# Two convolution blocks in one kernel: another order of work at the seams between its passes

## The chip, the cores and the metric

The kernel runs on one core of one Trainium2 chip. A core has a matrix engine (TensorE, PE in the profile, with weight loads listed apart as PEld), a vector engine (VectorE, DVE), an activation engine (ScalarE, ACT), a general engine (GpSimd, POOL) and a queue engine (SyncE, SP) that only issues transfers. Each engine works through its own instructions in order. Transfers are issued from SP, ACT or POOL and run on 16 DMA engines. The metric is the time of one execution on the device, in microseconds (us); lower is better.

## The reference, cut to what matters

The input x is an image batch of shape (8, 96, 96, 192) in f32. Two layers follow each other, both with a residual sum:

```python
x = x + L0(group_norm(x, 32 groups))      # layer 0
x = x + L1(group_norm(x, 32 groups))      # layer 1

def L0(x):                                # 192 -> 384 -> 192 channels
    proj  = x @ W_in + b_in
    local = depthwise_conv_3x3(proj)
    # s = 0.6 s + 0.4 v, along the width and the height, both ways
    mixed = 0.25 * (lr + rl + tb + bt) + local
    return (layer_norm(mixed) * ln_g + ln_b) @ W_out + b_out

def L1(x):                                # 192 -> 768 -> 192 channels
    y = depthwise_conv_7x7(x) + dw_bias
    y = layer_norm(y) * ln_gamma + ln_beta
    y = gelu(y @ w0 + b0)
    return (y @ w1 + b1) * gamma
```

Group norm needs the mean and the variance of a whole image over six channels before it can scale the first value, so layer 1 cannot begin with an image before layer 0 is done with it.

## The kernel before, in words

The work is cut into passes; what one pass leaves for the next goes through DRAM in another layout.

The **first pass** (0 to about 770 us) normalises x, multiplies by W_in and writes P_d.

The **second pass** (770 to 1,820 us) goes over the 384 channels in 96 steps of four (k), each in three parts (i). A part is loaded (`load_b`), convolved 3x3 on TensorE (`conv_b`), scanned down and up on VectorE (`scan_down`, `scan_up`), mixed on TensorE (`mix_b`), and the scans are added to the mix by GpSimd (`add`, L672). The mix of a step trails its convolution by one step. Every second step, a tile mo of 8 channels is full, and eight transfers (`store_steps`, L655) write it to M_d, two per part of the following step, all issued by GpSimd. After the last step the rest is issued at once.

The **third pass** (1,842 to 2,652 us) takes 192 units, one image column and one half of the batch each. `load_c` loads mt (the column of M_d, all 384 channels, 576 KB) and xr (the column of x, 288 KB), three units ahead, on SP. `block_c` transposes and multiplies by W_out on TensorE, `finish_c` scales and adds x. Sixteen units fill a tile x1c, which is stored to X1_d by twelve transfers (`store_c`, L1034) on SP, one per unit; after the last unit all twelve go out together. Statistics for layer 1's group norm are taken on the way. For the first half of the batch they are finished inside the pass; for the second half by the six steps of `norm_c(1)` later. Twenty units before the end, band 0 and raw 0, the first inputs of the 7x7 convolution, are loaded.

The **7x7 convolution** has 32 steps: two batch halves times 16 groups of 12 channels (`todo`). A step needs the following:
- `load_raw(n, t)`, t = 0 to 2: one tile of X1_d each, of which SP and GpSimd load 64 partitions each (384 KB a half).
- `load_band(n)`: the band matrices (624 KB) for 64 partitions, by SP for an even n and by GpSimd for an odd one; VectorE copies them to the other 64 (`spread`, L817).
- `scale_steps(n)`: 24 scale operations (L806) from raw into xin, the group norm, and `spread` behind them.
- `conv_d(n, c)`, c = 0 to 5: 24 matmul instructions (L1131) and two ScalarE evictions into yo.
- `store_d(n)`: six transfers into Y_d, half of them on SP and half on GpSimd.

Tiles alternate between two pools, `early` and `d_own`, so that a step's inputs load while the step before computes; d_own opens after the third pass, in memory that the third pass used, and raw 1 belongs to early. Steps 0 to N1 - 1 run in a loop of their own ahead of the last pass; the other steps are cut into nine slots each and run inside the last pass's first half.

The **last pass** (3,010 us to the end) has 72 units (u), two per tile y. `load_y` reads Y_d (four transfers on SP), `load_r` reads X1_d for the residual, and GpSimd adds the bias to it (`bias_r`, L1190). `prepare` and the pieces of it in the loop take the layer norm's statistics and write yn on VectorE, with a power on GpSimd (L29). `turn_in(u, k)` transposes yn on TensorE (L1226) into the only buffer of its PSUM pool, and VectorE copies that to yT (L1229). `first_layer` multiplies by w0 (L1244, L1254), with Gelu on ScalarE; `second_layer` multiplies by w1 (L1274), and VectorE adds the residual (L1285). Unit u's first layer stands beside unit u - 1's second layer. In the first half (`early_half`) a unit's first layer comes in three parts with five PSUM banks, in the second in two parts.

The order is written out by hand: inside a block opened by `tc.manual_schedule()` each engine gets its instructions in the order of the source. Between blocks, instructions of a later one can move up where an engine would be free: SP issues its halves of raw 1 at 2,616 and 2,635 us, inside the third pass. Waits are put in by the framework, by tile.

Of the kernel before, what the change touches and what calls it, by code (L numbers as in the profile page):

```python
# [101 lines left out]
def conv_blocks_kernel(  # L102
# [51 lines left out]
    M_d = dram.tile([S, C, B, S], F32, name="M_d")  # L154
# [406 lines left out]
    with ExitStack() as ph:  # L561
# [81 lines left out]
        def store_steps(mo, o):  # L643

            steps = []
            for i in range(NI):
                runs = []
                for at, (c, j) in enumerate(place[i]):
                    if runs and runs[-1][1] == c:
                        runs[-1][3] += 1  # L650
                    else:
                        runs.append([at, c, j, 1])
                for at, c, j, n in runs:
                    steps.append(
                        lambda i=i, at=at, c=c, j=j, n=n: nc.gpsimd.dma_start(  # L655
                            M_d[
                                j * RB : (j + n) * RB, o * 2 * CC + c : (o + 1) * 2 * CC : CC
                            ].rearrange("w c b h -> w c (b h)"),
                            mo[at * RB : (at + n) * RB, :, i].rearrange("p k q n -> p k (q n)"),
                        )  # L660
                    )
            return steps

        n_k = C // CC
        with tc.manual_schedule():
# [3 lines left out]
            def add(k, i):  # L669
                m = mos[k // 2][:, k % 2, i].rearrange("p q (j n) -> p q j n", j=3)  # L670
                z = zs.pop((k, i)).rearrange("p q (n j) -> p q j n", j=3)
                nc.gpsimd.tensor_tensor(m, m, z, ALU.add)  # L672

            up_next = None
            for n in range(NI * (n_k + 1)):
# [18 lines left out]
                if k:  # L694
# [7 lines left out]
                    if k % 2 and i == NI - 1:  # L702
                        todo += store_steps(mos.pop(k // 2), k // 2)
# [57 lines left out]
    N1 = NI + 2  # L761
# [33 lines left out]
    def scale_steps(n):  # L795
# [4 lines left out]
        def scale(t, k, b):  # L800
            if (t, k, b) == (0, 0, 0):
# [4 lines left out]
            nc.vector.tensor_scalar(  # L806
                xins[n][:, t, b, c].rearrange("q c (a v) -> q a c v", a=NV),
                raws[n, t][:, b, :, c],
                sc,
                sh,  # L810
                ALU.mult,
                ALU.add,
            )
# [86 lines left out]
    with ExitStack() as ph:  # L900
# [48 lines left out]
        M_f = M_d.rearrange("w c b h -> w c (b h)")  # L949
# [6 lines left out]
        def load_c(u):  # L956
# [4 lines left out]
            nc.sync.dma_start(  # L961
                mt,
                M_f[S - 1 - w, :, hf * NH * S : (hf + 1) * NH * S].rearrange(
                    "(m c) n -> c m n", c=128
                ),
            )
# [487 lines left out]
```

## Time and profile before

| what | us |
|---|---|
| median of three runs | 5,662.74 (5,660.78 to 5,672.44) |
| the profiled execution's own time | 5,654.68 |
| its span, first to last instruction | 5,652.9 |
| TensorE busy | 5,393.8 (95% of the span) |
| VectorE, ScalarE, GpSimd busy | 3,066.6, 2,233.1, 2,103.9 |
| first matmul of the third pass (L979) | at 1,841.5 |
| first matmul of convolution step 1 (L1131) | at 2,696.3 |
| first matmul of the last pass's first layer (L1244) | at 3,016.3 |

The mean granted TensorE clock is 0.979 of full speed. The profile's rows are read like this: a number of an L is a line of the kernel; `out<-in` names the tiles that an instruction writes and reads; an arrow with an engine and a line names what ended a wait. In the slices the span is cut into 40 equal parts of 141 us, and a digit is the busy share in tenths. In a timeline row the first number is the start and the second the length from the first to the last instruction of a merged group, and the brackets give the idle time of the engine before it. A releaser is inferred, and where a wait had several causes the last one is named.

### The profile page before, as it was taken

The page shows a single profiled execution, that of the slowest core. Times are in us where ns is not written, and L with a number is a line of the kernel's source. Part 1 is how long each engine was busy: PE and PEld are TensorE (multiplying, and loading weights), DVE is VectorE, ACT ScalarE, POOL GpSimd, SP SyncE. Part 2 cuts the span into 40 slices and gives each one's busy share as a digit, 9 for nine tenths or more (in the row PEclk, how much of TensorE's full clock was granted, in tenths as well). Part 3 has the DMA queues.
Part 4 walks back from the last instruction along what each step waited for, and adds up shares of the span by engine and source line. Part 5 has one row for each costly group of instructions (what it writes and reads, how often), then busy time and mean ns, then how long its engine had stood idle before and what let it go on. Part 6 is the DMA issues. An engine that isn't in the chain of part 4 may idle for free.

```text
span 5652.9 us, 106714 instructions
## 1 busy us (share of the span) xinstructions
PE 5393.8 (95%) x43070; PEld 3443.0 (61%) x43070; DVE 3066.6 (54%) x6353; ACT 2233.1 (40%) x5282; POOL 2103.9 (37%) x2093
## 2 busy tenths in 40 slices
PE   5999989999998999997688999999999999999999
PEld 3666643333332999997344666666666667676777
DVE  5556449999998455554545444444333334333332
ACT  2444447777775566564232222222222222222221
POOL 1111128888888555554222222222222222222221
PEclk9999989999999999999789999999999999999999
DMA  7999869999997899999898456555332222322321
GB/s 200 283 285 272 238 196 243 243 245 242 244 246 206 256 285 289 281 288 265 217 274 196 117 106 129 126 126 123 86 74 67 69 69 69 80 69 69 72 65 40
DMA packets 695589, 996.62 MB, mean 176 GB/s; under 512 B 234343, under 2 KB 576920, under 8 KB 693048
## 3 DMA queue, kind: packets, MB, share of 16 engines
q1 hardware_dynamic: 598600, 620.64, 44.8%
q0 software_dynamic: 90368, 366.55, 20.8%
q8 instruction: 340, 5.57, 0.4%
q10 hardware_dynamic: 6128, 2.61, 0.2%
q14 instruction: 153, 1.25, 0.1%
HBM read 585.22 MB, written 419.95 MB: 178 GB/s over the span
## 4 chain that ended last, share of the span: by engine, by line
PE 77%; DMA 4%; issue 2%; DVE 2%; POOL 1%; SPq 0%; ACT 0%; POOLq 0%; DVEq 0%; ACTq 0%
PE hp L1274 19%; PE hp L1244 13%; PE pl L599 11%; PE po L981 11%; PE hp L1254 7%; PE pa L620 5%; PE hp L1131 4%; PE pt L979 3%; PE pa L623 2%; PE pt L1226 2%; DMA raw<-X 1%; DMA band<-Z_d 1%; DVE xin L806 1%; DMA Y<-yo 1%; DMA mt<-M_d 0%
## 5 line engine op out<-in xcount | busy, mean ns | idle before, releaser
L1274 PE MATMUL hp<-w1g,g 128*128 128x192 f32 x6912 | 1170.8, 328 | 4.0 <-DVE xo L1285 4.0
L1263 ACT ACTIVATE g<-hp,b0g 128x512 f32<-128x512 f32 x864 | 519.8, 692 | 1641.9 <-PE hp L1254 1641.9
L1274 PEld LDWEIGHTS hp<-w1g,g 128*128 128x128 f32 x6912 | 1121.2, 190 | 68.6 <-issue 42.5
L1293 POOL DMA_DIRECT2D out_dram<-xo x288 | 211.3, 734 | 1613.9 <-DVE xo L1285 1579.6
L1244 PE MATMUL hp<-yT,w0w 128*128 128x512 f32 x1728 | 779.3, 597 | 0.0
L981 PE MATMUL po<-wc,mt 128*128 128x193 f32 x3456 | 685.0, 334 | 1.8 <-DVE x1c L998 1.8
L599 PE MATMUL pl<-pin,band 34*32 34x380 f32 (+1 forms) x13824 | 631.1, 490 | 18.8 <-DMA pin<-P_d 18.5
L1285 DVE TENSOR_TENSOR xo<-hp,r 128x384 f32<-128x384 f32 x288 | 230.6, 801 | 739.3 <-PE hp L1274 739.3
L672 POOL TENSOR_TENSOR mo<-mo,z 128x768 f32<-128x768 f32 x288 | 602.1, 2091 | 2.9 <-ACT mo L624 0.4
L981 PEld LDWEIGHTS po<-wc,mt 128*128 128x128 f32 x3456 | 554.8, 191 | 32.3 <-ACT mean L983 30.1
L1229 DVE COPY yT<-pt 128x512 f32<-128x512 f32 x216 | 148.8, 689 | 749.6 <-PE pt L1226 749.5
L1244 PEld LDWEIGHTS hp<-yT,w0w 128*128 128x128 f32 x1728 | 320.3, 191 | 358.4 <-issue 353.4
L632 DVE TENSOR_TENSOR_SCAN z<-decay,loc 128x768 f32<-128x768 f32 x288 | 505.9, 1756 | 45.4 <-ACT loc L608 16.7
L1131 PE MATMUL hp<-xin,band 63*64 63x372 f32 (+1 forms) x4608 | 430.0, 509 | 101.2 <-DVE band L817 51.8
L641 DVE TENSOR_TENSOR_SCAN z<-decay,z 128x768 f32<-128x768 f32 x288 | 498.4, 1731 | 0.1
L599 PEld LDWEIGHTS pl<-pin,band 34*32 34x32 f32 x13824 | 232.5, 107 | 399.1 <-issue 398.2
L1141 ACT ACTIVATE yo<-hp,dwb 128x384 f32<-128x384 f32 x384 | 202.2, 578 | 608.2 <-PE hp L1131 443.2
L620 PE MATMUL pa<-loc,mix 128*32 128x384 f32 x3456 | 432.8, 494 | 0.0
L623 PE MATMUL pa<-last,down 96*32 96x384 f32 x1152 | 427.7, 494 | 0.9 <-ACT mo L624 0.9
L1254 PE MATMUL hp<-yT,w0w 64*128 64x512 f32 x1728 | 419.5, 611 | 0.0
L381 PE MATMUL pm<-xT,win 128*128 128x384 f32 x1152 | 394.4, 493 | 8.0 <-DVE po L405 8.0
L1131 PEld LDWEIGHTS hp<-xin,band 63*64 63x64 f32 x4608 | 211.6, 141 | 278.7 <-issue 244.7
(141 smaller groups left out, 6674.4 us busy)
## 6 DMA issues: line engine op xcount, KB each, us to landing
P_d<-po POOLq DMA_DIRECT2D x96, 1152.0 KB, 9.8
pin<-P_d SPq DMA_DIRECT2D x192, 576.0 KB
mt<-M_d SPq DMA_DIRECT2D x192, 576.0 KB
xq<-in_x_dram SPq DMA_DIRECT2D x96, 576.0 KB
xr<-in_x_dram SPq DMA_DIRECT2D x192, 288.0 KB
X<-x1c SPq DMA_DIRECT2D x144, 384.0 KB
y<-Y SPq DMA_DIRECT2D x144, 384.0 KB
r<-X SPq DMA_DIRECT2D x36, 1536.0 KB
```

Of the source, the lines that this page charges most:

```text
L599: nc.tensor.matmul(pls[g][at * RB : (at + 1) * RB, :, lo:hi], band[rows, c, kh, :], pin[rows, c, :, NJ - 1 - j, lo + kh - 1 : hi + kh - 1] ...
L620: nc.tensor.matmul(pa[at], mix[:, i, at], loc[:, q], start=True, stop=True)
L623: nc.tensor.matmul(pa[at], down[:, to], last[:, q], start=True, stop=True)
L632: nc.vector.tensor_tensor_scan(zf, decay_f, loc.rearrange("p q n -> p (q n)"), 0.0, ALU.mult, ALU.add)
L641: nc.vector.tensor_tensor_scan(zr, decay_f, zr, 0.0, ALU.mult, ALU.add)
L672: nc.gpsimd.tensor_tensor(m, m, z, ALU.add)
L981: nc.tensor.matmul(po, lhs[m], wc[:, m], start=(m == 0), stop=(m == NC - 1))
L1131: nc.tensor.matmul(pys[g][k * 64 : (k + 1) * 64, :, lo:hi], band[rows, k * GS + c, d * ZS : d * ZS + 64], xin[rows, :, :, k * GS + c, lo + ...
L1244: nc.tensor.matmul(hps[m, q], w0w[:, 2 * q, m * 128 : (m + 1) * 128], yT[:, 2 * q], start=True, stop=False,)
L1254: nc.tensor.matmul(hps[m, q], w0w[p, 1, m * 128 : (m + 1) * 128], yT[p, 1], start=False, stop=True,)
L1263: nc.scalar.activation(g[:, m, q], hps[m, q], AF.Gelu, bias=b0g[:, m : m + 1], scale=1.0)
L1274: nc.tensor.matmul(po[:, q], g[:, m, q, k * 128 : (k + 1) * 128], w1g[:, m], start=(m == 0), stop=(m == NE - 1),)
```

## The change

It moves work over the seams between the passes, and changes two tensors and a count.

- M_d becomes two DRAM tensors, one for the first 256 channels and one for the last 128, and `load_c` loads mt with two transfers.
- In the second pass's last step, VectorE does the adds of parts 1 and 2 in place of GpSimd, and each part's stores are issued right behind its add, by SP and GpSimd in turn.
- `load_raw(1, t)` moves from the start of the convolution's loop to the end of the third pass, ahead of its last stores; step 1's scale operations move from VectorE to ScalarE.
- N1 is 19 instead of 18, so one step more runs ahead of the last pass. `load_y(1)`, the next step's band and its raw move behind the last convolution of that loop; `load_y(0)` stays at step 16, and `prepare(0)` at the last step.
- The six steps of `norm_c(1)` go one by one to steps 3 to 8 instead of three each to steps 1 and 2; `make_weights` goes from step 2 to step 10, ahead of the scale operations.
- In the last pass slots begin with unit 2 instead of unit 0, `load_y(2)` stands behind `prepare(1)`, and in the first half `turn_in(u + 1, 1)` stands ahead of `second_layer(u - 1, 1)` instead of behind it.

The core of the diff (the loop that builds the runs in `store_steps` is only un-nested):

```diff
-    M_d = dram.tile([S, C, B, S], F32, name="M_d")
+    CS = 2 * C // 3
+    M_d = [dram.tile([S, n, B, S], F32, name=f"M_{n}") for n in (CS, C - CS)]
...
-        def store_steps(mo, o):
+        def store_steps(mo, o, i, engs=(nc.gpsimd,)):
+
+            m, lo = divmod(o * 2 * CC, CS)
...
+            for at, c, j, n in runs:
+                eng = engs[len(steps) % len(engs)]
+                steps.append(
+                    lambda eng=eng, at=at, c=c, j=j, n=n: eng.dma_start(
+                        M_d[m][
+                            j * RB : (j + n) * RB, lo + c : lo + 2 * CC : CC
+                        ].rearrange("w c b h -> w c (b h)"),
+                        mo[at * RB : (at + n) * RB, :, i].rearrange("p k q n -> p k (q n)"),
                     )
+                )
...
-                nc.gpsimd.tensor_tensor(m, m, z, ALU.add)
+                eng = nc.vector if k == n_k - 1 and i else nc.gpsimd
+                eng.tensor_tensor(m, m, z, ALU.add)
...
-                    if k % 2 and i == NI - 1:
-                        todo += store_steps(mos.pop(k // 2), k // 2)
+                    if k == n_k - 1:
+                        for step in todo + store_steps(
+                            mos[k // 2], k // 2, i, (nc.sync, nc.gpsimd)
+                        ):
+                            step()
+                        todo = []
+                    elif k % 2 and i == NI - 1:
+                        for i in range(NI):
+                            todo += store_steps(mos[k // 2], k // 2, i)
...
-    N1 = NI + 2
+    N1 = NI + 3
...
-            nc.vector.tensor_scalar(
-                xins[n][:, t, b, c].rearrange("q c (a v) -> q a c v", a=NV),
-                raws[n, t][:, b, :, c],
-                sc,
-                sh,
-                ALU.mult,
-                ALU.add,
-            )
+            to = xins[n][:, t, b, c].rearrange("q c (a v) -> q a c v", a=NV)
+            of = raws[n, t][:, b, :, c]
+            if n == 1:
+                nc.scalar.activation(to, of, AF.Identity, bias=sh, scale=sc)
+            else:
+                nc.vector.tensor_scalar(to, of, sc, sh, ALU.mult, ALU.add)
...
-            nc.sync.dma_start(
-                mt,
-                M_f[S - 1 - w, :, hf * NH * S : (hf + 1) * NH * S].rearrange(
-                    "(m c) n -> c m n", c=128
-                ),
-            )
+            for f, m in zip(M_f, (slice(0, CS // 128), slice(CS // 128, NC))):
+                nc.sync.dma_start(
+                    mt[:, m],
+                    f[S - 1 - w, :, hf * NH * S : (hf + 1) * NH * S].rearrange(
+                        "(m c) n -> c m n", c=128
+                    ),
+                )
...
                 held = (pos, var, xr) if u < n_u else None
+            for t in range(NT):
+                load_raw(1, t)
             for store in stores:
                 store()
...
             load_band(1)
-            for t in range(NT):
-                load_raw(1, t)
             norms = norm_c(1, bank)
             for n in range(N1):
                 if n:
                     store_d(n - 1)
-                    load_band(n + 1)
+                    if n + 1 < N1:
+                        load_band(n + 1)
                 if n == NI:
                     load_y(0)
-                    load_y(1)
+                if n >= 3 and norms:
+                    norms.pop(0)()
+                if n == 10:
+                    make_weights(bank())
                 if n == N1 - 1:
-                    for t in range(NT):
-                        load_raw(N1, t)
                     prepare(0)
...
-                if n == 2:
-                    make_weights(bank())
                 for c in range(GS):
                     conv_d(n, c)
-                    if 0 < n < 3 and c % 2:
-                        norms.pop(0)()
+            load_y(1)
             store_d(N1 - 1)
+            load_band(N1)
+            for t in range(NT):
+                load_raw(N1, t)
...
-            if slots:
+            if slots and u >= 2:
                 for step in slots.pop(0):
                     step()

         load_r(0)
-        load_y(2)
         for k in range(3):
             turn_in(0, k)
         prepare(1)
+        load_y(2)
...
             if early_half:
                 first_layer(u, 1, parts, pool)
+                turn_in(u + 1, 1)
             second_layer(u - 1, 1, pool)
-            turn_in(u + 1, 1) if u < n_u else None
+            if not early_half and u < n_u:
+                turn_in(u + 1, 1)
             slot()
```

More of the change, by code (lines that the diff above doesn't have):

```diff
@@ L641, in scan_up @@
             nc.vector.tensor_tensor_scan(zr, decay_f, zr, 0.0, ALU.mult, ALU.add)
-        def store_steps(mo, o):
[L645 to L659, printed above, removed]
-                        )
+        def store_steps(mo, o, i, engs=(nc.gpsimd,)):
+            m, lo = divmod(o * 2 * CC, CS)
+            runs, steps = [], []
+            for at, (c, j) in enumerate(place[i]):
+                if runs and runs[-1][1] == c:
+                    runs[-1][3] += 1
+                else:
+                    runs.append([at, c, j, 1])
+            for at, c, j, n in runs:
[6 more added lines that the diff above has]
+                        mo[at * RB : (at + n) * RB, :, i].rearrange("p k q n -> p k (q n)"),
                     )
+                )
             return steps
@@ L805, in scale @@
             sc, sh = (s1[:, hf, b, e, 2 * i + k : 2 * i + k + 1] for e in range(2))
-            nc.vector.tensor_scalar(
-                xins[n][:, t, b, c].rearrange("q c (a v) -> q a c v", a=NV),
-                raws[n, t][:, b, :, c],
-                sc,
-                sh,
-                ALU.mult,
-                ALU.add,
-            )
+            to = xins[n][:, t, b, c].rearrange("q c (a v) -> q a c v", a=NV)
+            of = raws[n, t][:, b, :, c]
+            if n == 1:
+                nc.scalar.activation(to, of, AF.Identity, bias=sh, scale=sc)
+            else:
+                nc.vector.tensor_scalar(to, of, sc, sh, ALU.mult, ALU.add)
         def spread():
@@ L947, in conv_blocks_kernel @@
             nc.vector.tensor_tensor(cst, bo, ps[:, D : 2 * D], ALU.add)
-        M_f = M_d.rearrange("w c b h -> w c (b h)")
+        M_f = [m.rearrange("w c b h -> w c (b h)") for m in M_d]
         x_f = x.rearrange("b h w c -> (b h) w c")
@@ L960, in load_c @@
             mt = ip.tile([128, NC, NH * S], F32, tag="mt", name="mt")
-            nc.sync.dma_start(
-                mt,
-                M_f[S - 1 - w, :, hf * NH * S : (hf + 1) * NH * S].rearrange(
-                    "(m c) n -> c m n", c=128
-                ),
-            )
+            for f, m in zip(M_f, (slice(0, CS // 128), slice(CS // 128, NC))):
[5 more added lines that the diff above has]
+                )
             xr = ip.tile([128, NJ3, D], F32, tag="xr", name="xr", bufs=5)
```

## The prediction

> **What bounds the kernel now.** I read the page's slices first: which engine is full where.
>
> ```profile
> PE   5999989999998999997688999999999999999999
> PEclk9999989999999999999789999999999999999999
> DMA  7999869999997899999898456555332222322321
> ```
>
> TensorE is full nearly everywhere. The one hole wider than a slice lies in slices 18 to 21, 2,650 to 3,010 us, where the first 18 of the 32 steps of the 7x7 convolution run alone; there DMA is full instead. So an edit is worth what it takes out of a TensorE wait, and in that hole what it takes out of a DMA gap. The table of waits, TensorE only, says which waits exist (total, times, longest):
>
> ```profile
> PE hp L1131 <- DVE band L817: 51.8, 10, 30.1
> PE hp L1131 <- DMA band<-Z_d: 35.7, 6, 8.5
> PE pt L979 <- DMA mt<-M_d: 28.7, 2, 21.2
> PE pt L1226 <- DVE yT L1229: 21.7, 21, 1.2
> PE hp L1131 <- DVE b0g L748: 9.3, 1, 9.3
> ```
>
> The change touches every one of these five. The same hole cut by time (time; busy of TensorE, weight loads, VectorE, ScalarE, GpSimd; clock; DMA share; GB/s):
>
> ```profile
> 2651.00:2768.00 117.00, 64.70 (x611) 33.20 (x612) 54.05 (x155) 25.27 (x48) 26.17 (x34) 0.75 0.78 197
> 2768.00:2980.00 212.00, 165.01 (x1750) 98.46 (x1752) 104.62 (x303) 75.81 (x144) 50.88 (x76) 0.87 1.01 275
> ```
>
> From step 4 on DMA is saturated at 275 GB/s and a step takes 17.3 us (from L1131's starts at 2767.6 and 2975.5, twelve steps), against 11.7 us of matmuls in a row. In the first 117 us DMA moves only 197 GB/s: that stretch is slack, not throughput.
>
> **1. End of the second pass.** GpSimd's timeline, and from the chain that ended last the third pass's first matmuls:
>
> ```profile
> 1813.12 5.98 POOL L672 TENSOR_TENSOR mo<-mo,z 128x768 f32<-128x768 f32 x3
> 1819.05 4.51 POOL L655 DMA_DIRECT2D M_d<-mo  x8
> ...
> 1841.47 0.90 PE pt L979 x3
> ```
>
> Three adds, then eight store issues, all on GpSimd; the chain then shows 9.3 us for the stores to land and 8.8 us for the first load of mt. After the change GpSimd has one of these adds, ending at 1815.2; VectorE, free of scans at 1811.1, does the other two. A 128x384 add of theirs (L859) takes 0.56 us, so 768 elements about 1 us each: done at 1813.1. Eight issues over two queues, five on SP and three on GpSimd at 0.56 us, end about 1818 instead of 1823.6. SP is free for them, having issued nothing since 1772. But the stores' 2.36 MB and 2 MB of weight loads already fill DMA until 1831, so landing gains about 4 us, not 5.6. Then only the last third of mt (192 KB) waits for it; the first two thirds are older and load meanwhile: 2 to 3 us more. Sum by the rows: -7 us.
>
> Here a rule speaks against the edit. A row shows VectorE and GpSimd in each other's way: eight scale operations, first without and then under a GpSimd operation of 5.44 us (L1190, started at 3242.67):
>
> ```profile
> 2771.72 2.41 DVE L806 TENSOR_SCALAR xin<-raw,s 128x192 f32<-128x192 f32 x8 [2.79 <-DMA raw<-X]
> ...
> 3242.12 8.13 DVE L806 TENSOR_SCALAR xin<-raw,s 128x192 f32<-128x192 f32 x8
> ```
>
> The Trainium skill (GPSIMD Engine Reference, 1. Specifications) says that GpSimd shares its SBUF interfaces with VectorE and contends with instructions that have two SBUF inputs, which these adds are. By the rule the adds run one after the other, about 2 us later, and the sum is -5. I take -6; bounds 0 and -11.
>
> **2. mt by two loads.** 192 more DMAs in the third pass (1,842 to 2,649 us, 4.13 us a unit, TensorE full, DMA 0.93 at 283 GB/s). SP issues mt in 0.36, xr in 0.55, a store in 0.60 us: with 0.4 more that is 1.9 of 4.13. The cover is a prefetch of three units. The rule against it: the skill (DMA: Bandwidth & Descriptors, Anatomy of one DMA) gives a fixed 2.0 us a DMA; exposed, 192 of them would be +384 us. But mt's loads carry such latencies already, and TensorE waited for mt just twice in the pass, so it is hidden unless it occupies the DMA engines. Bound for that: a unit moves 1.18 MB, which at 283/0.93 = 304 GB/s needs 3.88 us, slack 0.25. The second pass with its many small transfers (237 GB/s at share 0.91) keeps the engines 1.4 us longer per channel step of 10.9 us than 304 GB/s would, over 12 DMAs: 0.12 us each. Below 0.25: cost 0.
>
> **3. Start of the convolution.** TensorE's and GpSimd's rows:
>
> ```profile
> 2652.95 13.29 PE L1131 MATMUL hp<-xin,band 63*64 63x384 f32 x142 [2.77 <-DVE x1c L998]
> 2696.33 6.80 PE L1131 MATMUL hp<-xin,band 63*64 63x384 f32 x48 [30.09 <-DVE band L817]
> ...
> 2672.90 0.57 POOL L790 DMA_DIRECT2D band<-Z_d  x1 [21.40 <-DMA Y<-yo]
> 2673.47 3.74 POOL L780 DMA_DIRECT2D raw<-X  x6
> ```
>
> GpSimd's halves of step 1's raw stand behind the band load, which waits for memory that the third pass's last stores (4.7 MB, landing about 2,670) still hold. So VectorE scales at 2,687, and only then copies the band. Moved ahead of those stores, GpSimd's three issues go out at 2,651; SP's three went at 2,616 and 2,635 and stay. ScalarE scales as they land: 24 operations of about 0.37 us (0.16 for one element, L983, and 0.58 for 384, L985, give the line), 8.9 us. What queues behind: step 0's evictions on ScalarE, so step 0 ends near 2,675 instead of 2,667; nothing waits for that, as DMA is busy with the stores. The stores land some 4 us later for sharing; the band issues about 2,677 and lands about 2,684, and step 1 begins about 2,686, 10 us earlier. Then group norm and weight scaling leave steps 1 and 2, where they cost twice: 2.5 and 9.3 us of TensorE waits, and late stores behind which SP held the next loads (DMA share 0.07 in 2,710 to 2,720, 0.13 in 2,740 to 2,750). Spread over steps 3 to 8 and 10 they meet 17.3 - 11.7 = 5.6 us of idle TensorE a step; weight scaling takes 3.8 us of matmuls there, and VectorE reaches it ahead of the next band. GpSimd's powers (5.62 us) delays half a prefetched raw. The bytes check it: 23.0 MB in 2,651 to 2,768 take 84 us at 275 GB/s, 33 less than 117. I take -30; bounds -10 (step 1 alone) and -36.
>
> **4. A 19th step ahead of the last pass.** It adds 4.77 MB (raw 2.36, band 0.64, stores 1.77), 17.3 us at the stage's pace; out of the stage go y 1, the next band and raw, 4.6 MB. The end is a chain, not throughput. Count from step 15's start (before: 2,958.6). Its store lands about +32 (before +30; half a raw more beside it). SP, which waits there, then issues y 0 (1.57 MB), its half of raw 18, its half of store 16 and band 18: 5.2 MB, landed at +52. Copy, step 18 from +53.5 to +65.5, then three transposes with copies: first MLP matmul at +69.5. Before it came at 3,016.3, +57.7. So +11.8. y 0's statistics fit under step 18. Bounds +5 and +25.
>
> **5. The last pass.** One convolution step less inside: six pieces of 2.06 us (between neighbouring starts at 3,229.0 and 3,231.1), -12.4. And the moved turn_in:
>
> ```profile
> 4111.71 0.60 PE L1226 MATMUL pt<-ident,yn 128*128 128x128 f32 x4
> 4113.36 0.66 PE L1226 MATMUL pt<-ident,yn 128*128 128x128 f32 x4 [1.06 <-DVE yT L1229]
> ```
>
> Turns 1 and 2 follow each other and share one PSUM buffer; after 3,062 us this wait occurs 18 times, 19.0 us. With 4.1 us of second layer between them the 0.69 us copy is done. I take -19; bounds -21 and -10 (were VectorE late there). Next in line is the bank wait on L1285, 4.0 us in all, unchanged. The entry: before it idles 5.8 us after the first matmul and loses 3 to a cold clock (0.53 in 3,010 to 3,020). After, units 0 and 1 have no convolution to fill: 3.7 us for unit 1's yn, 1.1 for a turn pair, and about 5 for unit 2's yn, since GpSimd waits for r 0 before bias_r (5.4 us) and its power stands behind: +1 net, bounds -4 and +10. Slots 13 x 9 = 117 from unit 2 end in unit 25 as before.
>
> **Sum** against the profiled execution's 5,654.7 us (span 5,652.9 and 1.8 around it): -6 + 0 - 30 + 11.8 - 12.4 - 19 + 1 = -54.6, so 5,600. The median of the runs, 5,662.7, lies 8.1 higher; taken from it: **5,608 us**, 0.990 of before.
>
> **Rivals.** (a) A new wait in place of the old: step 0's evictions behind ScalarE's scaling, or scaling held by memory of the stores, so that step 1 stays at 2,696 and only the gaps of steps 1 and 2 go, some -12 instead of -30. For: xin 1 is in the same pool as band 1 and raw 2, which did wait for it (SP's raw 2 until 2,669.4). Against: raw 1 is in another, SP's halves of it landed before the stores, and even from 2,670 ScalarE would be done when the band lands. 5,626. (b) The end of the stage and the entry cost their upper bounds, +13 and +9: 5,630. For: SP waits in line with y 0. Against: GpSimd's queue runs on. (c) Gains add up fully: -11, -36, +5, -21, -4, with the step's -12.4 -79: 5,583. (d) Slower: the split loads make the third pass DMA-bound. At d us of engine time a DMA it costs 192 x (d - 0.25); the gain is gone at d = 0.53, four times my bound of 0.12. At d = 0.65, +77: 5,685. (e) The evicted waits were only symptoms of DMA throughput and the 19th step eats all: 3 gives 0, 4 +25, 5 stays, 1 gives 0: -5.4, so 5,657, no change.
>
> **Numbers.** Likeliest 0.56, own range 5,590 to 5,625; (a) 0.17; (b) 0.10; (c) 0.10; (d) 0.04; (e) 0.03. Range for 8 in 10: 5,584 to 5,638. Faster or slower counts beyond 0.2% (11 us), about what a measurement of this kernel can tell from no change: (d) is slower, (e) the same, the rest faster, 0.93, 0.03, 0.04.
>
> **What would show it.** Right: TensorE's wait on mt at the second pass's end down from 21.2 to about 15; step 1 at about +33 us from step 0 instead of 44, and 275 GB/s from there; the wait on L1229 almost gone after the entry; a late-half unit unchanged at 33.1 us. Wrong: DMA gaps that move to step 16 or to the entry; a third pass longer than 4.13 us a unit; ScalarE holding step 0 past 2,685.

## The result and the profile after

The changed kernel takes 5,613.0 us in the median (5 runs, 5,607.2 to 5,630.8), the kernel before, run beside it, 5,662.7 (5 runs, 5,653.0 to 5,674.3). The ratio is 0.9915 with a 95% interval of 0.9891 to 0.9939. The forecast was 5,608, with a range of 5,584 to 5,638. The profiled execution of the changed kernel took 5,613.0 us, its span 5,611.2, 41.7 less than the span before. Behind line 640 the line numbers are up to ten higher than in the kernel before: L1131 is now L1141, L1226 is L1236, L1229 is L1239, L979 is L987, L672 is L674; in the variants they differ by a few more.

The page's slices of the changed kernel:

```profile
PE   5999989999999999998777999999999999999999
...
PEclk9999989999999999999888999999999999999999
DMA  7999869999998899999997456555332223332321
```

The hole of TensorE is still there. In its second slice (about 2,665 to 2,806 us; 2,685 to 2,826 before) the DMA row was 8 and is 9; in the last slice of the hole it is 7. The table of waits of TensorE (total, times, longest) has these rows for the edits:

```profile
PE hp L1141 <- DMA band<-Z_d: 38.2, 6, 14.2
PE hp L1141 <- DVE band L824: 27.5, 11, 7.5
PE pt L987 <- DMA mt<-M: 27.4, 3, 18.1
...
PE pt L1236 <- DVE yn L1219: 11.8, 8, 8.1
PE hp L1141 <- ACT yo L1151: 8.4, 2, 7.3
...
PE pt L1236 <- DVE yT L1239: 2.4, 3, 0.8
```

The copied band cost 51.8 us before and costs 27.5. The wait for the yT copy is gone but for the entry. The wait for the weights' tile b0g (9.3) has no row any more. Two waits are new or longer: 14.2 us for one band, 7.3 us for one eviction. The wait on mt at the end of the second pass fell only from 21.2 to 18.1, not to 15. The convolution stage cut by time, columns as in the table of before:

```profile
2650.00:2768.00 118.00, 84.06 (x867) 41.44 (x868) 59.10 (x167) 48.11 (x96) 33.76 (x44) 0.84 0.99 270
2768.00:2945.00 177.00, 140.11 (x1472) 83.28 (x1471) 90.08 (x263) 63.07 (x120) 43.41 (x65) 0.87 1.01 275
2945.00:3005.00 60.00, 44.05 (x444) 20.29 (x445) 27.49 (x78) 20.20 (x37) 9.82 (x14) 0.80 0.87 214
```

The first stretch is now as full of DMA as the second: 270 GB/s at a share of 0.99, before 197 at 0.78. The gap has moved to the end of the stage, where DMA has 0.87; the kernel before had 1.03 in its last 60 us there (2,956 to 3,016). The forecast had named a gap that moves to step 16 or to the entry as a sign of being wrong; this one lies between them (0.46 in 2,990 to 3,005).

I cut each profiled execution at five starts of TensorE work: the end of the last mixing matmul (L621), the first matmul of the third pass, convolution steps 0 and 4, and the first matmul of the first layer (FL). All are read from TensorE's timeline; step 0 is counted from its main block of matmuls (2,650.81 in the changed kernel), not from the two that come 3.6 us earlier, among the third pass's last. The stretch ahead of the first cut is left out, since no kernel here changes it, and it varied by 21 us with the granted clock (last section). Times in us:

| kernel | mix to third pass | third pass to step 0 | step 0 to 4 | step 4 to FL | FL to the end | steps ahead |
|---|---|---|---|---|---|---|
| before | 30.2 | 811.5 | 114.6 | 248.8 | 2,636.6 | 18 |
| as changed | 29.3 | 814.1 | 84.6 | 269.6 | 2,606.2 | 19 |
| e1, turn_in back | 29.6 | 813.1 | 84.2 | 263.3 | 2,626.7 | 19 |
| e2, 18 steps | 29.5 | 813.0 | 86.8 | 239.3 | 2,619.9 | 18 |
| e3, seam back | 31.0 | 812.9 | 84.3 | 262.1 | 2,602.6 | 19 |
| e4, start back | 28.4 | 813.7 | 105.3 | 277.8 | 2,603.7 | 19 |
| e5, stores on GpSimd | 25.2 | 813.7 | 85.1 | 267.4 | 2,603.0 | 19 |
| e6, raw 1 back | 29.0 | 812.9 | 90.6 | 268.8 | 2,603.9 | 19 |
| e7, norms back | 30.2 | 812.4 | 108.0 | 275.1 | 2,603.1 | 19 |
| e8, bias late | 29.3 | 814.0 | 86.2 | 265.5 | 2,592.4 | 19 |
| e9, band 18 on GpSimd | 28.3 | 812.8 | 83.0 | 276.0 | 2,606.8 | 19 |
| e10, best with 18 | 24.1 | 813.2 | 84.4 | 242.9 | 2,611.2 | 18 |
| e11, best with 19 | 29.0 | 810.2 | 83.3 | 270.7 | 2,592.5 | 19 |
| e12, scaling on VectorE | 28.5 | 811.2 | 85.0 | 266.9 | 2,603.3 | 19 |

Each row is one execution. Where a stretch is the same code, it agrees within about 4 us, except in "step 4 to FL", where the spread is 8 (262.1 to 269.6 in the changed kernel, e1, e3, e5, e8 and e12): a difference below these is not read. The kernel before was run beside each group of variants, with medians of 5,662.7 to 5,668.1 us, so a few us between the wholes of different groups are not read either. Between before and after the stretches give -0.9 + 2.7 - 30.0 + 20.8 - 30.4, and -3.9 from the part ahead of them, which no edit touches: -41.7.

The end of the second pass in the changed kernel, rows of the timelines of VectorE, GpSimd and SP in order of time:

```profile
1807.12 6.11 DVE L674 TENSOR_TENSOR mo<-mo,z 128x768 f32<-128x768 f32 x2
1809.23 2.96 POOL L674 TENSOR_TENSOR mo<-mo,z 128x768 f32<-128x768 f32 x1
1812.40 12.27 SPq L656 DMA_DIRECT2D M<-mo  x5
1812.48 1.72 POOL L656 DMA_DIRECT2D M<-mo  x3 [0.30 <-POOL mo L674]
1829.02 0.89 SPq L969 DMA_DIRECT2D mt<-M  x2
```

The second pass ended 3.9 us earlier in this execution than in that of before, so I count from the last mixing matmul (1,807.4; before 1,811.3). GpSimd's add ends at +4.8 and its stores at +6.8, about where the forecast had them (+3.9 and +6.7), VectorE's adds at +5.8 (forecast +1.8). But SP needs 12.27 us for five stores and ends at +17.3, later than the last store of before (+12.3). In the table of SP's waits these stores wait 3.2 us on a load of aff and 3.5 us on the load of b0g, both issued by ScalarE, and 2.5 us on a store: SP was free, but not free to issue. Both loads of mt then go out together, after SP has waited 2.1 us for a store of M to land; so the two thirds of mt that were ready long before did not load meanwhile, as the forecast had it. Whether they wait for M itself or for memory that the second pass still used isn't shown.

The start and the end of the convolution stage and the entry of the last pass, rows of TensorE and SP:

```profile
2665.74 8.85 PE L1141 MATMUL hp<-xin,band 63*64 63x384 f32 x70 [7.32 <-ACT yo L1151]
2679.24 14.67 PE L1141 MATMUL hp<-xin,band 63*64 63x384 f32 x144 [4.66 <-DVE band L824]
...
2957.37 9.06 SPq L1185 DMA_DIRECT2D y<-Y  x4
2966.55 3.65 SPq L789 DMA_DIRECT2D raw<-X  x3
2971.91 1.27 SPq L799 DMA_DIRECT2D band<-Z_d  x1
2986.25 15.48 PE L1141 MATMUL hp<-xin,band 63*64 63x384 f32 x144 [14.21 <-DMA band<-Z_d]
...
3044.19 0.45 PE L1236 MATMUL pt<-ident,yn 128*128 128x128 f32 x1 [8.07 <-DVE yn L1219]
```

Step 1 begins 28.4 us behind step 0 (2,650.81), although step 0 was held 7.32 us for ScalarE's scaling. At the end, SP issues y 0 and its half of raw 18 first, and band 18 only at 2,971.9; TensorE waits 14.21 us for it. At the entry, 8.07 us go to unit 2's yn.

### The profile page after: what moved, and what is told of

It is laid out like the page before. It is cut to its first block, busy times and chain, and to the rows that moved or that the text cites. A ratio compares the mean times of both kernels' runs of the same rounds, so it can differ in the third digit from the quotient of the medians.

```text
span 5611.2 us, 106882 instructions
## 1 busy us (share of the span) xinstructions
PE 5384.6 (96%) x43070; PEld 3433.2 (61%) x43070; DVE 3068.6 (55%) x6331; ACT 2241.1 (40%) x5306; POOL 2099.1 (37%) x2086
## 3 DMA queue, kind: packets, MB, share of 16 engines
q0 software_dynamic: 90064, 365.17, 20.8%
## 4 chain that ended last, share of the span: by engine, by line
PE 45%; DMA 4%; issue 2%; DVE 1%; POOL 0%; SPq 0%; ACT 0%; POOLq 0%; DVEq 0%; ACTq 0%
PE hp L1284 19%; PE hp L1254 13%; PE hp L1264 7%; PE hp L1141 4%; PE pt L1236 2%; DMA raw<-X 2%; DMA band<-Z_d 2%; DVE xin L820 1%; DMA r<-X 0%; DVE band L824 0%; DMA Y<-yo 0%; ACT xin L818 0%; POOL out_dram L1303 0%; SPq L789 0%; POOL r L1200 0%
## 5 line engine op out<-in xcount | busy, mean ns | idle before, releaser
L1284 PEld LDWEIGHTS hp<-w1g,g 128*128 128x128 f32 x6912 | 1123.1, 191 | 40.3 <-issue 19.3
L1239 DVE COPY yT<-pt 128x512 f32<-128x512 f32 x216 | 148.9, 689 | 926.9 <-PE pt L1236 926.8
L674 POOL TENSOR_TENSOR mo<-mo,z 128x768 f32<-128x768 f32 x286 | 598.6, 2093 | 2.9
L1141 PE MATMUL hp<-xin,band 63*64 63x372 f32 (+1 forms) x4608 | 428.5, 511 | 77.0 <-DMA band<-Z_d 38.2
L621 PE MATMUL pa<-loc,mix 128*32 128x384 f32 x3456 | 431.6, 493 | 0.0
L609 ACT COPY loc<-pl 128x384 f32<-128x384 f32 x576 | 248.1, 483 | 311.0 <-PE pl L600 311.0
```

Source lines behind the costliest of these rows:

```text
L621: nc.tensor.matmul(pa[at], mix[:, i, at], loc[:, q], start=True, stop=True)
L674: eng.tensor_tensor(m, m, z, ALU.add)
L1141: nc.tensor.matmul(pys[g][k * 64 : (k + 1) * 64, :, lo:hi], band[rows, k * GS + c, d * ZS : d * ZS + 64], xin[rows, :, :, k * GS + c, lo + ...
L1284: nc.tensor.matmul(po[:, q], g[:, m, q, k * 128 : (k + 1) * 128], w1g[:, m], start=(m == 0), stop=(m == NE - 1),)
```

## The experiments

All are edits of the changed kernel. The first four undo one part each.

**e1: turn_in back behind the second layer.**

```diff
                 first_layer(u, 1, parts, pool)
-                turn_in(u + 1, 1)
             second_layer(u - 1, 1, pool)
-            if not early_half and u < n_u:
+            if u < n_u:
                 turn_in(u + 1, 1)
```

> The changed kernel with one edit undone: in the first half of the last pass turn_in(u + 1, 1) stands behind second_layer(u - 1, 1) again. My theory (the two turns share one PSUM buffer, and the copy between them is exposed): TensorE's wait on L1239 behind VectorE's copy returns from 2.4 us to about 21 us in all, 1.0 us each, and the last pass, counted from its first first-layer matmul to the end, grows by 19 us (2,606 to 2,625). Rival (the wait moves elsewhere, for instance to the banks of the first layer): the wait returns, but the pass grows by less than 8 us.

Measured: 5,638.6 us, 0.9942 [0.992, 0.9964] of before. TensorE's waits have the row of before again:

```profile
PE pt L1236 <- DVE yT L1239: 22.4, 22, 1.1
```

The last pass takes 2,626.7 us; the eight kernels that share the changed kernel's last pass, itself among them, have 2,602.6 to 2,606.8, median 2,603.5. The move is worth 23 us, a little more than the waits it removes (20.0), and the wait that comes back is the one named: for the copy out of the one PSUM buffer.

**e2: 18 steps ahead of the last pass.**

```diff
-    N1 = NI + 3
+    N1 = NI + 2
```

> The changed kernel with N1 = 18: step 18 of the convolution goes back into the last pass, all else as changed. The forecast held the 19th step for neutral, +11.8 at the end of the convolution stage and -12.4 inside the last pass, so it expects the time of the changed kernel within 2 us. From the changed kernel's trace (from step 15's start to the first first-layer matmul 76.7 us, where 69.5 were forecast) I now expect the chain without that step to take about 54 us and the last pass 12.4 more: about 10 us faster than the changed kernel. Rival (the 19th step is there to free d_own's memory early): residual 0 and the Gelu tiles wait for the last store from d_own, the entry of the last pass loses 10 to 15 us, and the kernel is as slow as the changed one or slower.

Measured: 5,602.7 us, 0.989 [0.9859, 0.9922]. The intervals overlap with those of the changed kernel, so the whole alone doesn't settle it; the stretches do. Step 4 to FL is 239.3 instead of 262.1 to 269.6 (median of the six kernels named above 266.2), and the last pass 2,619.9 instead of 2,603.5. The 19th step costs about 27 ahead of the last pass and saves 16 in it; e10 below, again with 18 steps, repeats both (242.9, and 2,611.2 against 2,592.4 in e8 with 19). It loses about 10 us; the edit is no part of the gain.

**e3: the end of the second pass and the single mt as before.** All adds on GpSimd, the stores in one block behind them, one M_d, one load of mt.

```diff
-                eng = nc.vector if k == n_k - 1 and i else nc.gpsimd
+                eng = nc.gpsimd
...
-                    if k == n_k - 1:
-                        for step in todo + store_steps(...): step()
...
-    CS = 2 * C // 3
+    CS = C
```

> The changed kernel with the second pass's end and mt's loads as before: all adds and all of the last stores on GpSimd, issued after the last add, one M_d, one load of mt. The forecast put these edits at -6, so undoing them costs 6 us: from the last mixing matmul to the third pass's first matmul 35 instead of 29.3 us. What the changed kernel's trace suggests instead (SP's stores wait in turn for the weight loads that ScalarE issued, and VectorE's adds take 3.1 us each beside GpSimd's): the edits brought about 1 us there, and the split loads cost about 2 in the third pass, so undoing them changes the time by -2 to +2 us. If the 3.9 us by which the second pass ended earlier are due to the edits, they are lost again here.

Measured: 5,609.5 us, 0.9903 [0.988, 0.9926]. The seam takes 31.0 us (before 30.2; with the edits 28.3 to 30.2), the third pass 812.9 with one load of mt and 810.2 to 814.1 with two. So the seam edits are worth one or two us at most, less than executions differ by, and the whole, 3.5 us under the changed kernel, shows no gain from them; the 192 more transfers cost nothing that can be seen.

**e4: the start as before.** Raw 1 behind the third pass's stores, its scaling on VectorE, the norms in steps 1 and 2, the weight making in step 2.

```diff
-            for t in range(NT):
-                load_raw(1, t)
             for store in stores:
...
             load_band(1)
+            for t in range(NT):
+                load_raw(1, t)
...
-            if n == 1:
+            if n < 0:
                 nc.scalar.activation(...)
...
-                if n >= 3 and norms:
-                    norms.pop(0)()
-                if n == 10:
-                    make_weights(bank())
...
+                if n == 2:
+                    make_weights(bank())
                 for c in range(GS):
                     conv_d(n, c)
+                    if 0 < n < 3 and c % 2:
+                        norms.pop(0)()
```

> The changed kernel with the start of the convolution as before: raw 1 loaded behind band 1, step 1 scaled on VectorE, group norm in steps 1 and 2, weight scaling in step 2. My theory: from step 0's matmuls behind the third pass to step 4's start 114 us instead of 84.6, DMA near 197 GB/s in it instead of 270, and the whole 28 to 30 us slower than the changed kernel. Rival (the later steps would have caught up, the stage being DMA-bound): step 4 is late by 30, but step 15 and the end by less than 15.

Measured: 5,646.3 us, 0.9965 [0.9955, 0.9975]: 33 above the changed kernel by the medians, 28 by the ratios. Step 0 to 4 takes 105.3 us, between the two kernels and not the 114 of before; step 1 comes 36.3 behind step 0, not 43.4. Nine of the 30 us are not brought back by these three parts. Seven of them lie ahead of step 1: band 1 goes out 17.0 us behind step 0 instead of 19.9, and step 1 begins 19.4 behind that instead of 23.4. DMA moves 279 and 264 GB/s there, before 259 and 234; why isn't settled. From step 0 to FL e4 takes 383.1, five kernels with the start and the 19 steps as changed 346.4 to 354.2, median 351.6 (the changed one, e1, e3, e5, e8).

**e6 and e7: the start taken apart.** e6 undoes only the loads of raw 1 and their scaling, e7 only the norms and the weight making (both parts as in the diff of e4).

> Only the raw tiles of step 1 go back behind the first band load after the third pass, and VectorE scales that step again; the norms and the weight making stay spread over steps 3 to 12. The kernel with all three parts of the start undone took 105.3 us from step 0 to step 4 (84.6 as changed): 8 of the 20.7 up to step 1, 12.8 behind it. Theory (the early raw tiles carry the gain up to step 1, the spread norms the gain behind it): step 0 to 1 about 36 instead of 28.4, step 1 to 4 stays near 56, so step 0 to 4 about 93 and the whole 8 us above the changed kernel, about 5,621. Rival (the start is bound by the amount of data alone, in whatever order): step 0 to 4 stays near 85 and the whole at 5,613. Second rival (the raw tiles carry nearly all of it): step 0 to 4 about 104 and the whole 20 to 30 above, about 5,640.

> Only the norms go back into steps 1 and 2 and the weight making into step 2; the raw tiles stay early and ScalarE still scales step 1. Theory (each part carries its own stretch): step 0 to 1 stays near 28.4, the waits for the weights' tile and for a band return in steps 2 and 3, step 1 to 4 about 69 instead of 56, so step 0 to 4 about 97 and the whole 13 us above the changed kernel, about 5,626. Rival (raw tiles carry it all, the norms' loads have time enough once step 1 is early): step 0 to 4 near 85, the whole at 5,613.

Measured: e6 5,620.6 us, 0.9927 [0.9901, 0.9952], step 0 to 1 35.8, step 0 to 4 90.6: its theory holds. e7 5,646.0 us, 0.9966 [0.9954, 0.9978], step 0 to 1 28.4, step 0 to 4 108.0: step 1 stays early as expected, but the loss is 33 us and not 13. Undoing the norms and the weight making costs as much as undoing all (step 0 to FL 383.1 in both). Step 1's row in e6:

```profile
2700.77 9.68 PE L1139 MATMUL hp<-xin,band 63*64 63x384 f32 x97 [24.23 <-DVE band L824]
```

In e6 TensorE waits 24.2 us ahead of step 1, where the changed kernel waits 12.0 (7.32 and 4.66). Step 1 comes 7.4 later, step 4 6.0 and FL about 8, at the edge of what these stretches resolve; the queues hardly notice, as DMA moves 283 GB/s in the 40 us behind step 0 and 287 in the changed kernel. In e7 the rows of VectorE, TensorE and GpSimd show why an early step 1 is worth nothing:

```profile
2692.60 1.45 DVE L824 COPY band<-band 64x2496 f32<-64x2496 f32 x1 [6.53 <-DMA band<-Z_d]
2694.08 0.66 DVE L852 TENSOR_REDUCE gn_ms<-gn_st 128x32 f32<-128x384 f32 x1
2694.88 0.60 PE L854 MATMUL hp<-gn_ms,blk 128*128 128x32 f32 x2 [11.92 <-DVE gn_ms L852]
...
2702.78 5.45 POOL L880 TENSOR_TENSOR gn_rb<-gn_ve,neg_half 128x32 f32<-128x32 f32 x1 [23.46 <-DVE gn_ve L877]
...
2709.95 0.58 POOL L799 DMA_DIRECT2D band<-Z_d  x1
```

VectorE waits for band 2 to land and copies it; the norm's first reduction stands behind that copy, and TensorE, in the middle of step 1, behind the reduction. So step 1 waits for step 2's data. Store 1 can go out only behind step 1, and the next loads stand behind it on both queues: SP's half goes out at 2,707.54 instead of 2,695.02, and band 3's load at 2,709.95 instead of 2,697.53. GpSimd's power, although it stands ahead of GpSimd's half, costs little, since that goes out at 2,708.19, 0.65 us behind SP's. Meanwhile DMA has little to do (share 0.17 from 2,700 to 2,710). For 2,690 to 2,770, e7 and then the changed kernel:

```profile
2690.00:2770.00 80.00, 56.84 (x546) 27.49 (x550) 31.08 (x87) 21.03 (x40) 18.46 (x21) 0.78 0.78 190
```

```profile
2690.00:2770.00 80.00, 58.85 (x642) 27.40 (x638) 39.53 (x109) 28.38 (x54) 25.64 (x32) 0.88 1.01 265
```

The 75 GB/s between them over 80 us are 6.0 MB, 22 us at 275 GB/s: that is about the difference in step 0 to 4 (108.0 and 84.6, so 23.4). The norms and the weight making were not undone singly. By the trace 16.8 of the 23.4 us lie between the starts of steps 1 and 2 (32.6 instead of 15.8), where the norms' chain is and 3.8 us of the weight making's matmuls, and 6.8 between those of steps 2 and 3, where TensorE waits 9.34 us for the weights' tile b0g. Here a TensorE wait cost what it did to the queues.

**e12: only the scaling of step 1 back on VectorE.**

```diff
-            if n == 1:
+            if n < 0:
                 nc.scalar.activation(...)
```

> Only the scaling of step 1 goes back from ScalarE to VectorE; raw 1 stays early and the norms stay spread. As changed, ScalarE was busy 10.62 us with the scaling and TensorE waited 7.3 us in step 0 for its evictions. Theory (with raw 1 early, either engine has time): the 7.3 us wait goes, step 1 waits instead for VectorE's 24 operations; step 0 to 4 stays within 4 us of 84.6, the whole within 3 us. Rival (VectorE's queue was the reason that step 1 was late, as the forecast had it): step 0 to 1 about 36, step 0 to 4 about 92, the whole 6 to 8 us slower.

Measured: 5,610.5 us, 0.991 [0.9893, 0.9928], step 0 to 1 29.3, step 0 to 4 85.0. The engine makes no difference; ScalarE's scaling took 10.6 us in the changed kernel (one operation every 0.44 us, forecast 8.9 in all) and the 7.3 us that TensorE waited for it in step 0 cost nothing, as did the wait for the band (16.0 us the longest) that came in its place. So what e6 lost, it lost by the loads of raw 1.

**e5: the last stores all from GpSimd.**

```diff
-                            mos[k // 2], k // 2, i, (nc.sync, nc.gpsimd)
+                            mos[k // 2], k // 2, i
```

> The last stores of the second pass all go out from GpSimd instead of from GpSimd and SP in turn; the two adds stay on VectorE and the stores still go at the step that fills them. As changed, SP's five stores left at 1,812.4 to 1,824.4 us, each behind transfers that ScalarE had issued, GpSimd's three by 1,814.2. Theory (SP's waits ate the gain): the last store leaves before 1,819, the stretch from the last mixing matmul to the first matmul of the third pass falls from 29.3 to about 25, the whole 4 us lower. Rival (the stretch is set by the landing of the weights' and stores' bytes, not by who issues them): 29 again, no change of the whole.

Measured: 5,621.5 us, 0.993 [0.9907, 0.9953]. The second pass ended 20 us later in this profiled execution than in that of the changed kernel, so times are counted from its last mixing matmul (1,827.5; as changed 1,807.4). GpSimd and SP in e5:

```profile
1832.52 4.51 POOL L656 DMA_DIRECT2D M<-mo  x8 [0.29 <-POOL mo L674]
...
1845.27 1.12 SPq L969 DMA_DIRECT2D mt<-M  x2
```

The last store is issued by +9.5 instead of +17.3 us, the first load of mt at +17.8 instead of +21.6. The stretch is 25.2 us, 24.1 in e10, but 29.0 in e11, all three with these stores. In e10, e5 and e11 that load is issued alike, at +18.5, +17.8 and +18.4, and the third pass begins 5.6, 7.5 and 10.6 us later: what differs is the landing, as the rival had it. In e5 and e11 the load of mt itself waits for a load of aff that ScalarE issued (10.3 us of the chain that ended last in e11). The early issue of the stores is shown; that it brings 4 us is seen in two of three executions, and the whole does not show it.

**e8: the first bias add behind unit 0's work.**

```diff
         load_y(2)
-        bias_r(0)
...
+            if u == 0:
+                bias_r(0)
             second_layer(u - 1, 3, pool)
```

> The first bias add into the residual tile, which made GpSimd wait 23.96 us for that tile and TensorE 8.07 us for unit 2's normalized tile, moves behind the work of unit 0, just ahead of its last second layer. Theory: the 8.07 us wait goes; from the first first-layer matmul to the end 2,606.2 becomes about 2,599, the whole 6 to 8 us lower. Rival (the residual tile lands so late that the wait only moves to GpSimd's next tile): the wait comes back at unit 3's tile or at the output add, the whole within 2 us of the changed kernel.

Measured: 5,603.4 us, 0.9894 [0.9865, 0.9922]. The last pass takes 2,592.4 us, 11 less than the median of 2,603.5, and e11 repeats it with 2,592.5. Waits of TensorE at the entry in e8:

```profile
PE pt L1236 <- DVE yn L1219: 3.5, 4, 2.4
```

They were 11.8 us with a longest of 8.1. GpSimd had waited 24.0 us for r 0 with the power of unit 2 queued behind; theory confirmed, and larger than expected. The rest stands behind that wait: in the changed kernel four transposes take 2.5 us instead of e8's 0.66, each held up for its piece of yn, and the next part of the second layer 6.08 instead of 4.07, at a granted clock of 0.76 in 3,030 to 3,050 (1.00 in e8).

**e9: band 18 from GpSimd's queue.**

```diff
-        (nc.sync, nc.gpsimd)[g].dma_start(
+        (nc.sync, nc.gpsimd)[1 if n == N1 - 1 else g].dma_start(
```

> Only the last band before the last pass (band 18) is loaded by GpSimd's queue instead of SP's; SP had issued it 43.6 us behind step 15's start, after y 0's four loads and raw 18's half, and TensorE waited 14.21 us for it. Theory (the place in SP's queue made the end of the stage 7 us longer than forecast): the wait falls to 5 or less, step 18 begins about 50 us behind step 15 instead of 58, the whole 5 to 8 us under the changed kernel. Rival (the bytes ahead of it set its landing, not the queue): the wait stays at 12 to 14, or goes to the raw tile or to y 0's unit, and the whole stays within 2 us.

Measured: 5,620.9 us, 0.9926 [0.991, 0.9943]. The band is no longer what TensorE waits for, but the rival held: the wait went to raw 18 (the median is 8 us above the changed kernel's, with overlapping intervals). SP, GpSimd and TensorE in e9:

```profile
2978.03 12.04 SPq L1185 DMA_DIRECT2D y<-Y  x4
2978.11 0.55 POOL L799 DMA_DIRECT2D band<-Z_d  x1
2990.18 6.79 SPq L789 DMA_DIRECT2D raw<-X  x3
...
3007.55 1.51 PE L1141 MATMUL hp<-xin,band 63*64 63x384 f32 x2 [18.75 <-DVE xin L820]
```

SP's half of raw 18 stands behind y 0 just as the band did, and SP waits for stores of Y before it issues y 0 (19.3 us in its table of waits). Step 18 begins 65.6 us behind step 15, not 50 (58.9 in e11, which has the same edit). DMA is full through the wait (share 1.02 from 2,978 to 3,007.6), so step 18 waits for the bytes in line ahead, y 0's among them. That y 0 at that place delays the end of the stage is likely by these rows, but not shown: a version with y 0 behind both loads wasn't run.

**e10 and e11: what the runs pointed to.** e10 joins e2, e5 and e8; e11 joins e5, e8 and e9.

> The changed kernel with 18 steps ahead of the last pass as before, with the first bias add behind unit 0, and with the last stores of the second pass all from GpSimd. The parts measured singly: about 10 (18 steps), 10 (bias add, of the last pass's 2,603 to 2,592) and 4 (stores). Theory (they lie at three places and add up): 20 to 25 us under the changed kernel, about 5,590, 1.3% under the kernel before. Rival (without the 19th step the entry has the loads of y 0 and y 1 later, and the gain of the bias add is taken by another wait there): about 12 to 15 under, 5,600.

> The changed kernel with its 19 steps, with the first bias add behind unit 0, the last stores of the second pass all from GpSimd, and band 18 from GpSimd's queue. Theory (three places, they add up): 10 + 4 + 6, about 20 us under the changed kernel, about 5,593, within 5 us of the variant with 18 steps. Rival (band 18 gains nothing): about 14 under, 5,599.

Measured: e10 5,591.4 us (5,586.7 to 5,596.8), 0.9873 [0.9851, 0.9894], and e11 5,609.9, 0.9903 [0.9886, 0.9921]. e10 beats both kernels: its slowest run is 10 us under the changed kernel's fastest, though they ran on different chips and the two intervals of the ratio to before just touch. The gain over the changed kernel is 21.6 us by the medians, inside its theory. e11 missed: its last pass shows the 11 us of e8, but neither its seam (29.0) nor its step 4 to FL (270.7) gained.

## Why the prediction was right, and where it wasn't

The forecast of 5,608 lies 5 us under the median. By medians the change brought 49.7 us where the sum said 54.6. By the profiled executions it brought 41.7, 3.9 of them ahead of any edit. Term by term:

- **Part 1, the end of the second pass, -6: mis-sized, about -1.** The step that failed is "SP is free for them, having issued nothing since 1772". An engine with nothing to do was taken for one that can issue. SP's stores waited for ScalarE's loads, and the last left 17.3 us behind the last mixing matmul, where the forecast had 6.7. The 2 to 3 us for the older two thirds of mt failed too, as they went out no earlier than the rest. The rule that I weighed (the Trainium skill, GPSIMD Engine Reference, 1. Specifications: SBUF interfaces shared with VectorE) agrees with the trace: GpSimd's add beside VectorE's two took 2.96 us instead of 2.07, and VectorE's two took 6.11 together, where I had estimated 1 us each. That made VectorE 4 us later than forecast, still 11 us ahead of SP's last store, so it was not the loss.
- **Part 2, mt by two loads, 0: right** (e3). The rule weighed there (the Trainium skill, DMA: Bandwidth & Descriptors, Anatomy of one DMA, a fixed 2.0 us a DMA) is measured on transfers that GpSimd issues, while mt's go out from SP; whatever their fixed cost is, it lies hidden behind the prefetch: the third pass took 812.9 us with one load of mt and 810.2 to 814.1 with two.
- **Part 3, the start, -30: the size right, the split wrong.** Step 4 came 30.0 us earlier. Undoing the three parts (e4) gives back 20.7 of them; what brought the other nine is open. And I counted 10 for an early step 1 by itself and the rest for the norms, as if they added. The runs show 32 us from step 0 to FL for all three parts (383.1 against the median of 351.6 of five kernels), nothing for early raw with the norms left in place (e7), about 24 for the norms and the weight making alone (e6), and 8 for the raw tiles once these are out of the way. My reading of their cost (late stores, SP holding the next loads, DMA at 0.07 to 0.13) was the right one; e7 has such gaps again, 0.17 in 2,700 to 2,710 and 0.25 in 2,730 to 2,740. Rival (a) is out: step 1 came even earlier than I said, at +28.4 instead of +33, and step 0's eviction wait did no harm.
- **Part 4, the 19th step, +11.8: mis-sized, +19.0** (step 15 to FL 76.7 instead of 57.7). The chain was the right one, y 0 and raw 18 ahead of band 18 on SP. The step that failed is "5.2 MB, landed at +52". SP began to issue y 0 at +29.1, but until band 18 had landed, at +57.9, DMA moved 7.6 MB. (The items listed there come to 4.3 MB; 5.2 counts the whole of store 16.) So step 18 began at +58.0, not +53.5, and from there to FL it took 18.8, not 16: behind its wait the clock was 0.80, and its matmuls took 15.5 us. The whole edit, which I had as neutral (+11.8 - 12.4), loses about 10 (e2).
- **Part 5, the last pass, -30.4: the sum right to the tenth by chance, its terms not.** Eight executions have -33 in the median. The convolution step is worth 16 by e2, not 12.4, turn_in 23, not 19. The entry is the mis-sized term: to close the sum at -33 (2,636.6 to the median of 2,603.5) it must cost 6 more than before, where I wrote +1. The traces show these 6: the first two units take 76.8 us before, with one convolution step (12.4) inside, and 70.4 to 71.0 in the eight kernels, with none. The mechanism stood in the forecast, GpSimd waiting for r 0 with a power behind it; I gave it about 5 us, it took 8.07 with some 4 more behind it, and e8 gained 11 by removing it. Together with part 4 that is about half of what rival (b) had (+13 and +9). The late-half unit is unchanged, 33.1 us. Rivals (d) and (e) are out: the third pass is as before, and the waits were no mere symptoms of throughput, as the start shows.

So the number came out because the misses, 5 at the seam, 9 from step 4 to FL and 3 in the third pass's one execution, less 4 that came from the clock ahead of all edits, are small beside the two gains that held, the start and turn_in; that the terms of the last pass cancelled was luck.

## What to carry to other kernels

In a stage that is bound by DMA, judge an edit by whether the transfers' issue goes on without a gap, not by the length of a TensorE wait: here a wait of 16 us that came in place of one of 7 cost nothing (e12), and one of 12 us was part of a chain that cost 23 (e7). Keep small statistics work out of the instruction streams that also release the next loads, or put it ahead of the operation that waits for a transfer; one reduction behind a band copy tied step 1 to step 2's data. Before an engine or queue is counted as free, look at what its next instruction would wait for, with every transfer in line ahead of it, those of other queues too.

## What the runs showed of the hardware that I had not expected

**The clock after an idle gap.** TensorE idles twice for about 9 us between the first and the second pass (767 to 787 us in the changed kernel), and afterwards it stays at half clock for a time that differs from one execution to the next, with the same code. The row 820 to 830 us of e5 and of the changed kernel (clock is the third number from the end):

```profile
820.00:830.00 10.00, 10.00 (x96) 2.52 (x96) 5.60 (x4) 5.01 (x12) 2.51 (x3) 0.50 0.12 26
```

```profile
820.00:830.00 10.00, 10.00 (x192) 3.39 (x184) 9.68 (x7) 6.96 (x18) 6.67 (x8) 1.00 0.87 178
```

Both have a busy TensorE from 790 us on. The clock is back at 1.00 from 810 us on in the changed kernel, from 820 in the kernel before (0.96 in the ten before), and only from 850 in e5. By then e5 is 19.6 us behind the changed kernel (its fifth channel step begins at 852.7 instead of 833.1), and its second pass ended 20.1 us later. In the clock records of the 14 traces the half clock there lasts 34.1 us (four times), 41.0, 47.8, 54.6 (twice), 61.4, 68.3 (three times), 75.1 or 81.9, so in steps of 6.8 us, and the end of the second pass moves with it, from 1,806.4 to 1,827.5. The Trainium skill (TensorE: Matmul & The Clock Gate, Part 1: The HAM clock gate) gives about 3.4 us of sustained activity until the full clock; here it took 17 us (changed kernel), 24 (before) and 64 (e5) of a TensorE that the profile shows as busy. What sets the number of steps isn't shown. Two profiles of this kernel can so differ by 20 us ahead of any change, and only stretches, or medians of several runs, can be compared.

**Stores behind another engine's loads.** SP's stores waited 3.2 and 3.5 us on loads that ScalarE had issued and whose data they do not need; GpSimd issued eight such stores in 4.51 us without a wait. The trace's records show why. A transfer tells of its landing by a semaphore (a counter), and in this program SP and ScalarE use eight of these together, in turn, and GpSimd eight of its own. Ahead of each of these stores the queue waits until the earlier transfer with the same semaphore has landed: the stores issued at 1,816.03 and 1,824.35 have those of ScalarE's loads of aff (1,812.13) and b0g (1,820.52).

**VectorE beside GpSimd.** In the second of the two rows that the forecast showed for this (3,242.12, eight scale operations in 8.13 us) only the first operation is slow: it takes 6.11 us and ends at 3,248.2, when GpSimd's operation ends (3,248.1); the other seven take 0.36 to 0.37 each. One operation was held for the whole of GpSimd's, the rest lost nothing.
